# The last stage of a four-stage kernel: every engine's queue written out in the source's order, the scores one round earlier, the second layer's weights in single steps

## The chip, the cores and the metric

The kernel runs on one core of a Trainium2 chip. A core has five engines with a queue each: TensorE (PE in the profile), VectorE (DVE), ScalarE (ACT), GpSimd (POOL) and SyncE (SP), which here issues DMAs. The metric is the device time of one execution in microseconds (us). The kernel before took 1390.21 us (median of 3 runs, 1388.39 to 1392.13).

## The reference, cut to what matters

Two sequences of 1024 tokens of width 128 pass through four blocks, each added to its input after a layer norm: an attention, a mixture of experts, a second attention, and last a two-layer transformer with local attention. Only this last block is touched by the change:

```python
def _layer(x, wqkv, qs, ksc, wo, lg, lb, w1, b1, w2, b2):
    h = shift_token(x)                      # half of the features come from the token before
    q, k, v = jnp.split(h @ wqkv, 3, axis=-1)   # 8 heads of 64
    q = l2norm(q) * qs
    k = l2norm(k) * ksc
    q, k = rotary_xpos(q, k)
    o = local_attention(q, k, v)            # windows of 64, each sees itself and the one before
    x = x + o @ wo
    h = layernorm(shift_token(x)) * lg + lb
    a, g = jnp.split(h @ w1 + b1, 2, axis=-1)
    return x + (a * gelu(g)) @ w2 + b2
for l in range(2):
    x = _layer(x, ...)
```

## The kernel before

Four functions, `phase1` to `phase4`, do the four blocks. The change lies in `phase4` and in one new helper. `phase4` works on tiles of 128 tokens: 2 layers x 2 sequences x 8 tiles make 32 tiles, numbered n = 0 to 31 (`where`, L1152). A loop (L1441 to L1464) runs over rounds i; in each round a list of stages is called, each for the tile that is `late` rounds behind. One round of the list is what is called a round below.

The stages of one tile, with the lateness of each before:

- `stage_a` (0, L1159): q and k from the shifted tokens, six matmuls of 512 columns in two PSUM banks. From each bank ACT takes squares (`acc`, L1172), then DVE two products with the rotary tables (`rot` L1174 and `t` L1177).
- `stage_a1` (0, L1180): POOL adds the two products for q and for k (L1183); DVE sums the squares per head (`ss`, L1185); POOL clips them (L1186).
- `stage_a2` (1, L1189): ACT takes Ln, Exp and Square of the sums (L1193 to L1196); DVE makes the inverse norms (`rz`, `rn`, L1197 and L1198).
- `stage_b0` (2, L1201): POOL scales q and k (L1208); ACT casts k, q and a zero-padded q called Z to f16 (L1148).
- `stage_b1` (2, L1217): DVE and POOL make the f16 remainders (`q` L1222, `k` L1223); SP issues three transposing DMAs, Qz from Z, K from k, Q from q (L1229 to L1231).
- `stage_b2` (2, L1234): the values; ACT copies V (L1148), SP issues two DMAs that make a shifted copy Vs (L1245, L1247).
- `stage_c` (3, L1251): first pass of the scores, DVE takes row maxima (`mz`, L1272). ACT carries half of this tile's K into the buffer of the next tile, times a factor (L1277, called the carry below). It is absent for the last tile of a sequence.
- `stage_c2` (4): the maxima transposed into one small PSUM bank `sm`, and copied by ACT to `mT`. `stage_d` (4, L1288): the scores again, 40 small matmuls, and two Exp of ACT (`p`, L1303). `stage_e` (4, L1306): values weighted; DVE divides (L1323, L1324).
- `stage_e1` (5): the output transposed, copied by ACT (`oT`, L1333). `stage_f` (6): output projection, added by DVE to `F` (L1343).
- `stage_g` (L1345): the feed-forward part, for groups that end at the tiles in `ENDS`: seven groups of four tiles, then two of two. It is a generator: a `yield` cuts it into steps, and each `advance` runs one step of every open group. Its costly steps are the gelu (L1396, with a load of ACT's tables before and after, the latter by `exp_tables`, L68), the products (L1404), the way back (L1410 to L1417) and for the second layer a layer norm and the output.
- `stage_x` (L1074): at every fourth round the shifted, transposed tokens of four coming tiles, through the same bank `sm`: ACT and DVE take turns on it (L214, L215).

The second layer's weights and the second sequence's first layer norm are generators too (`weights` L1036, `normalize` L1028); they are put on the same list of generators as `stage_g` at rounds 12 and 4.

The order of work before: PE alone is held to the order of the source. `in_line` (L129) chains its instructions by an edge without a semaphore (`chain`, L121). ACT's table users have a chain of their own, and the carry is kept in program order. Every other instruction of DVE, ACT, POOL and SP is placed by the scheduler, which puts whatever it finds ready first.

PSUM: seven banks go round (`bank`, L1105), the eighth is `sm`.

Of the kernel before, what the change touches and what calls it, by code (L numbers as in the profile page):

```python
# [29 lines left out]
class Core:  # L30
# [98 lines left out]
    def in_line(self, f, *args):  # L129

        traced = self.nc.cur_bb.bb.instructions
        start = len(traced)
        r = f(*args)
        self.chain("line", [i for i in traced[start:] if i.engine == ENGINES[0]])
        return r
# [860 lines left out]
def phase4(k, X):  # L996
# [8 lines left out]
    with ExitStack() as es:  # L1005
# [22 lines left out]
        def normalize(b):  # L1028
            x = [X[:, NT * b + t, :] for t in range(NT)]
            mv, rstd = k.ln_stats(cp, lambda t: x[t])  # L1030
            yield
            k.ln_to(cp, [F[b][:, t, :] for t in range(NT)], lambda t: x[t], mv, rstd, scalar=b == 1)
# [3 lines left out]
        def weights(l, own, work):  # L1036

            def split(pool, name, shape, dt, src, **kw):
                w = work(shape)
                nc.sync.dma_start(w, src)  # L1040
                nc.gpsimd.tensor_scalar(w, w, WS, None, ALU.mult)
                h, lo = pool.tile(shape, dt, name=name + "h"), pool.tile(shape, dt, name=name + "l")
                nc.scalar.copy(h, w)
                nc.gpsimd.tensor_tensor(lo, w, k.f(h) if dt == F32R else h, ALU.subtract)
                return h, lo

            wq = split(own, "wq", [128, 1024], F16, A["L1_ffn_wqkv"][l][:, 0:1024])
            yield
            wv = split(own, "wv", [128, 512], F16, A["L1_ffn_wqkv"][l][:, 1024:1536])
            yield  # L1050

# [4 lines left out]
            for j in range(4):  # L1056
                nc.gpsimd.tensor_tensor(tab[:, j], tab[:, j], qs[:, j // 2, j % 2, :].unsqueeze(1).to_broadcast([128, NT, HD]), ALU.mult)
            yield
# [4 lines left out]
            w1 = split(own, "w1", [128, 6, D], F16, A["t_f1"][l])  # L1063
            col = own.tile([128, 9], F32, name="col")
            nc.sync.dma_start(col, A["t_col4"][l])
            nc.gpsimd.tensor_scalar(col[:, 0:3], col[:, 0:3], WS, None, ALU.mult)
# [26 lines left out]
        yield from weights(0, cp, work0)  # L1093
# [15 lines left out]
        class FromBank:  # L1109
            tile = staticmethod(lambda shape, dt, name: bank())  # L1110
        def from_bank(shape, dt):
            t = bank()
            if dt == F16:
                t = t.bitcast(F16)
            return t[:, :shape[1]]
        from_sm = lambda shape, dt: ps_sm.tile(shape, dt, name="sm")
        SRC = {'c2': 0, 'f': 1, 'g': 1, 'x': 0}
        src_c2 = from_bank if SRC["c2"] else from_sm
        src_f = from_bank if SRC["f"] else from_sm
        src_g = from_bank if SRC["g"] else from_sm  # L1120
        src_x = FromBank if SRC["x"] else ps_sm
# [20 lines left out]
        ENG = {'kc': 'a', 'qh': 'a', 'kh': 'a', 'z': 'a', 'oh': 'd', 'ql': 'd', 'kl': 'p', 'ul': 'd', 'gl': 'd', 'ol': 'p', 'qn': 'p', 'kn': 'p', 'uh': 'a', 'gh': 'd', 'fl': 'd', 'v': 'a', 'ra': 'p', 'rb': 'p', 'lnh': 'a', 'lno': 'd', 'mt': 'a'}  # L1142
        EDGE = {'ol': 'p', 'qh': 'a'}
        SPAN = (0, 30)
        engine = lambda n, i: ENG[n] if SPAN[0] <= i < SPAN[1] else EDGE.get(n, ENG[n])
        eng = lambda n, i=8: {"a": nc.scalar, "d": nc.vector, "p": nc.gpsimd}[engine(n, i)]
        def cpy(n, dst, src, i=8):
            (nc.scalar.copy if engine(n, i) == "a" else eng(n, i).tensor_copy)(dst, src)  # L1148

        keep = k.tc.keep_in_program_order  # L1150
# [29 lines left out]
        def stage_a1(i):  # L1180
            rot, t2, sq = S.pop(("a", i))
            for j in (1, 0):
                eng("ra" if j else "rb", i).tensor_tensor(rot[:, j], rot[:, j], t2[:, j], ALU.add)  # L1183
            ss = ep.tile([128, 2 * H], F32, name="ss")
            nc.vector.tensor_reduce(ss, sq.rearrange("p j h d -> p (j h) d"), AX.X, ALU.add)  # L1185
            nc.gpsimd.tensor_scalar(ss, ss, 1e-24 * WS**2, None, ALU.max)  # L1186
            S["a1", i] = rot, ss

        def stage_a2(i):  # L1189
            rot, ss = S.pop(("a1", i))  # L1190
            y = ep.tile([128, 2 * H], F32, name="rn")
            z = ep.tile([128, 2 * H], F32, name="rz")
            ln = nc.scalar.activation(z, ss, AF.Ln)  # L1193
            exp = nc.scalar.activation(y, z, AF.Exp, scale=-0.5)
            k.chain("tables", [ln.ins, exp.ins])
            nc.scalar.activation(z, y, AF.Square)  # L1196
            nc.vector.scalar_tensor_tensor(z, z, -0.5, ss, ALU.mult, ALU.mult)  # L1197
            nc.vector.scalar_tensor_tensor(y, z, 1.5, y, ALU.add, ALU.mult)  # L1198
            S["a2", i] = rot, y

        def stage_b0(i):  # L1201
            l, b, t = where(i)
            k0 = i % RK
            rot, rn = S.pop(("a2", i))
            rf = rot.rearrange("p j h d -> p (j h) d")
            for e, en in ((1, "kn"), (0, "qn")):
                r = slice(H * e, H * e + H)
                eng(en, i).tensor_tensor(rf[:, r, :], rf[:, r, :], rn[:, r].unsqueeze(2).to_broadcast([128, H, HD]), ALU.mult)  # L1208
# [3 lines left out]
            cpy("qh", mid(q16), pair(q), i)  # L1212
            cpy("kh", ends(k16), pair4(kk), i)
            cpy("z", ends(Z[i % 2]), pair4(q))
            S["b", i] = rot, q16, k16

        def stage_b1(i):  # L1217
            l, b, t = where(i)
# [3 lines left out]
            eng("ql", i).tensor_tensor(ends(q16), pair4(q), mid4(q16), ALU.subtract)  # L1222
            eng("kl", i).tensor_tensor(mid4(k16), pair4(kk), ends(k16), ALU.subtract)  # L1223
            if t == 0:
                nc.gpsimd.memset(K[k0][:, :, 0:64], 0.0)
            Q = sp.tile([128, H, 128], F16, name="Q", bufs=QB)
# [7 lines left out]
        def stage_b2(i):  # L1234
# [9 lines left out]
            cpy("v", V[v0][:, :, 0:HD], heads(pv), i)  # L1244
            nc.sync.dma_start(Vs[v0][64:128, :, :], V[v0][0:64, :, :])  # L1245
            if t < NT - 1:
                nc.sync.dma_start(Vs[v1][0:64, :, :], V[v0][64:128, :, :])  # L1247

        bc4 = lambda ap: ap.unsqueeze(1).to_broadcast([128, 4, 128])

        def stage_c(i):  # L1251
# [22 lines left out]
            if t < NT - 1:  # L1274
                dst = K[(i + 1) % RK][:, :, 0:64]
                if ENG["kc"] == "a":
                    keep(nc.scalar.activation(dst, K[k0][:, :, 128:192], AF.Copy, scale=fac[:, t : t + 1]))  # L1277
                else:
                    keep(nc.vector.tensor_scalar(dst, K[k0][:, :, 128:192], fac[:, t : t + 1], None, ALU.mult))

        def stage_c2(i):
            ps = src_c2([128, 128], F16)
            nc.tensor.transpose(ps, S.pop(("z", i)), k.ident16)
            mT = mTs[2] if where(i)[2] == 0 else mTs[i % 2]
            cpy("mt", mT[0:H, :], ps[0:H, :], i)
            S["m", i] = mT

        def stage_d(i):  # L1288
# [4 lines left out]
            for g in range(2):  # L1293
# [9 lines left out]
                k.chain("tables", [nc.scalar.activation(p[:, 4 * g : 4 * g + 4], st, AF.Exp).ins])  # L1303
# [32 lines left out]
        def stage_f(i):  # L1336
# [3 lines left out]
            ps = src_f([128, D], F32)  # L1340
# [4 lines left out]
        def stage_g(l, b, t0, T, last):  # L1345
# [5 lines left out]
            bank1 = bank if last else lambda: src_g([128, 512], F32)  # L1351

            def place(name, other):
                if last:
                    t = sq_place if other == "sq" else ep.tile([128, 2, H, HD], F32, name=other, bufs=3 if other == "rot" else 2)
                    return t.rearrange("p j h d -> p (j h d)")[:, :512]
                return sp.tile([128, 512], F32, name=name, bufs=1)

            tiles = lambda ap: ap[:, :n].rearrange("p (t d) -> p t d", d=D)
            hc = tiles(place("hc", "rot"))  # L1360

            ps = bank1()[:, : 64 * T].rearrange("p (t d) -> p t d", d=64)
# [11 lines left out]
            if ENG["lnh"] == "a":  # L1374
                k.ln_scalar(sp, [hc[:, t, :] for t in range(T)], mv, rstd)
            else:
                for t in range(T):
                    k.ln_apply(hc[:, t, :], hc[:, t, :], mv, rstd, t)
            yield
            yield  # L1380
            ps = bank1()
            for t in range(T):
                nc.tensor.transpose(ps[:, 128 * t : 128 * t + 128], hc[:, t, :], k.ident)
            hg = place("hc", "t2")[:, :n]
            nc.scalar.activation(hg, ps[:, :n], AF.Identity, scale=col[:, 7:8], bias=col[:, 8:9])
            gh = sp.tile([128, 512], F16, name="gh", bufs=1)[:, :n]
            gl = sp.tile([128, 512], F16, name="gl", bufs=1)[:, :n]
            nc.scalar.activation(gh, ps[:, :n], AF.Identity, scale=col[:, 7:8], bias=col[:, 8:9])
            (nc.vector if last else eng("gl")).tensor_tensor(gl, hg, gh, ALU.subtract)
            yield  # L1390
            ges = []
            for i in range(3):
# [4 lines left out]
                k.chain("tables", [gelu.ins])  # L1397
                ges.append(ge)
            k.exp_tables(gelu)
            yield  # L1400
            for i, u in enumerate(ges):
                pa = bank("g")[:, :n]
                k.mm3(pa, w1h[:, i, :], w1l[:, i, :], gh, gl)
                nc.vector.scalar_tensor_tensor(u, pa, col[:, i : i + 1], u, ALU.add, ALU.mult)  # L1404
            yield
            if not last:
                yield
            py = bank1()[:, :n]
            for i in range(3):
                nc.tensor.matmul(py, w2[:, i, :], ges[i], start=i == 0, stop=i == 2)  # L1410
            yT = place("hc", "sq")[:, :n]
            nc.scalar.activation(yT, py, AF.Identity, bias=col[:, 6:7], scale=1 / WS)
            yield
            ps = tiles(bank1())
# [230 lines left out]
```

## Time and profile before

| what | value |
|---|---|
| runs before | 1390.21 us median of 3 (1388.39 to 1392.13) |
| the profiled execution | 1389.02 us, its span 1387.2 us |
| first `rot` (L1174) of the last stage | 991.5 us |
| squares of tile 31 (L1172) start | 1309.0 us |
| Exp of tile 31 (L1303) start | 1350.5 us |
| F of tile 31 (L1343) start | 1364.9 us |
| PE, DVE, ACT, POOL busy in the whole span | 84%, 75%, 70%, 62% |

The last stage thus fills some 395 us of the span, from 991.5 us on. The time of an execution is its span and 1.8 us that lie around it. Of the views, "busy by stretches" gives each engine's busy time in a stretch of the span with the granted clock of PE, "one line" gives how often a line of the source ran, between which times and how long, and "instructions in order of time" gives start, duration, engine, line, output and input.

### The profile page before, as it was taken

The numbers are of one execution on the slowest core, as the hardware profiler recorded it, in microseconds if no ns is written. First come the engines' busy times: TensorE is split into PE (matmuls) and PEld (weight loads), VectorE is DVE, ScalarE is ACT, GpSimd is POOL, SyncE is SP. The second block draws the span as 40 slices with busy tenths as digits, with TensorE's granted clock in tenths as the row PEclk, the third lists the DMA queues.
The fourth block names the chain that finished last, engine by engine and source line by source line (L and its number), as shares of the span: only waits on it lengthen the run. The fifth ranks groups of instructions, "written<-read, shape, count | busy, mean of one in ns | idle before, by whom it ended". The sixth has DMA issues, their size and how long they took to land.

```text
span 1387.2 us, 28450 instructions
## 1 busy us (share of the span) xinstructions
PE 1159.8 (84%) x11534; PEld 729.5 (53%) x11534; DVE 1045.9 (75%) x2029; ACT 973.0 (70%) x1494; POOL 863.2 (62%) x536
## 2 busy tenths in 40 slices
PE   4789999999889687776998987689648888988986
PEld 1356666666556565544444443344325655655664
DVE  6776666876662688979978889775679887888854
ACT  2777777887667484641888876579757878887755
POOL 1666667777667363744576677576797786666611
PEclk7999999999999898987999999799959999999998
DMA  2000000010000211200000021000077755545530
GB/s 75 1 2 2 2 2 1 2 32 2 2 1 18 74 48 60 81 19 2 5 3 5 6 52 24 12 8 1 5 149 130 128 104 105 99 98 96 102 61 16
DMA packets 122530, 56.75 MB, mean 41 GB/s; under 512 B 105216, under 2 KB 114320, under 8 KB 122400
## 3 DMA queue, kind: packets, MB, share of 16 engines
q1 hardware_dynamic: 119920, 53.53, 18.3%
q8 instruction: 90, 1.47, 0.4%
q10 hardware_dynamic: 1472, 1.09, 0.3%
q0 software_dynamic: 1008, 0.33, 0.2%
q14 instruction: 40, 0.33, 0.1%
HBM read 20.99 MB, written 1.11 MB: 16 GB/s over the span
## 4 chain that ended last, share of the span: by engine, by line
PE 40%; DVE 31%; ACT 14%; POOL 6%; issue 6%; DMA 2%; SPq 0%; POOLq 0%; DVEq 0%; ACTq 0%
DVE mx L865 6%; PE big L360 5%; PE pu L49 4%; PE pu L51 3%; PE pu L50 3%; DVE nm L332 3%; ACT pt L894 2%; PE pu L916 2%; PE big L49 2%; PE big L50 2%; PE big L51 2%; DVE hl L642 1%; PE bankz L856 1%; PE bank L891 1%; DVE F L92 1%
## 5 line engine op out<-in xcount | busy, mean ns | idle before, releaser
L367 POOL TENSOR_TENSOR hl<-p,hl 128x1024 f16<-128x1024 f32 x128 | 273.9, 2143 | 139.0 <-ACT hl L366 110.9
L899 POOL TENSOR_TENSOR hl<-pt,hl 128x2048 f16<-128x2048 f32 (+1 forms) x48 | 164.7, 3435 | 102.3 <-ACT hl L898 58.9
L332 DVE TENSOR_REDUCE nm<-big 128x2 f32<-128x1024 f32 x128 | 155.1, 1219 | 31.9 <-PE big L329 31.1
L364 ACT ACTIVATE p<-big 128x1024 f32<-128x1024 f32 x128 | 130.8, 1022 | 51.9 <-PE big L360 51.1
L49 PEld LDWEIGHTS <-hl 128*128 128x128 f16 x1024 | 100.5, 98 | 73.8 <-DVE acc L392 41.2
L366 ACT CAST hl<-p 128x1024 f16<-128x1024 f32 x128 | 133.8, 1045 | 4.1
L865 DVE TENSOR_REDUCE mx<-bankz 128x1 f16<-128x512 f32 (+3 forms) x156 | 99.6, 657 | 26.3 <-PE bankz L860 19.5
L894 ACT ACTIVATE pt<-bank 128x512 f32<-128x512 f32 (+1 forms) x173 | 97.3, 601 | 26.0 <-PE bank L893 11.8
L865 DVE TENSOR_REDUCE mx<-bank 128x1 f16<-128x512 f32 (+1 forms) x148 | 94.4, 654 | 18.2 <-PE bank L860 12.5
L1208 POOL TENSOR_TENSOR rot<-rot,rn 128x512 f32<-128x512 f32 x64 | 66.9, 1066 | 61.8 <-DVE rn L1198 44.8
L49 PE MATMUL pu<-V1h,hl 128*128 128x129 f16 x512 | 92.6, 224 | 12.4 <-DVE acc L392 11.1
L50 PEld LDWEIGHTS <-hl 128*128 128x128 f16 x1024 | 101.2, 99 | 0.0
L49 PE MATMUL pu<-V0h,hl 128*128 128x129 f16 x512 | 92.8, 224 | 9.2 <-DVE acc L392 7.5
L51 PEld LDWEIGHTS <-hl 128*128 128x128 f16 x1024 | 100.3, 98 | 0.0
L894 ACT ACTIVATE pt<-bankz 128x512 f32<-128x512 f32 (+1 forms) x131 | 75.2, 597 | 35.8 <-PE bankz L893 29.4
L1183 POOL TENSOR_TENSOR rot<-rot,t 128x512 f32<-128x512 f32 x64 | 83.9, 1321 | 15.6 <-DVE t L1177 12.2
L50 PE MATMUL pu<-V0l,hl 128*128 128x129 f16 x512 | 92.1, 221 | 0.0
L51 PE MATMUL pu<-V0h,hl 128*128 128x129 f16 x512 | 92.1, 222 | 0.0
L51 PE MATMUL pu<-V1h,hl 128*128 128x129 f16 x512 | 92.0, 222 | 0.0
L50 PE MATMUL pu<-V1l,hl 128*128 128x129 f16 x512 | 92.0, 221 | 0.0
L898 ACT CAST hl<-pt 128x2048 f16<-128x2048 f32 (+1 forms) x48 | 78.4, 1634 | 10.1 <-PE pu L916 9.8
L891 PE MATMUL bank<-qst,kz 128*128 128x512 f16 (+3 forms) x222 | 66.7, 344 | 14.8 <-DVE mx L865 9.4
(418 smaller groups left out, 3797.9 us busy)
## 6 DMA issues: line engine op xcount, KB each, us to landing
sb<-sd SPq DMA_DIRECT2D x16, 512.0 KB, 4.1
Vs<-V SPq DMA_DIRECT2D x60, 130.0 KB, 2.4
work<-in_t_w SPq DMA_DIRECT2D x3, 512.0 KB, 3.6
out<-F SPq DMA_DIRECT2D x3, 256.0 KB, 2.3
X<-in_L_attn_x SPq DMA_DIRECT2D x2, 256.0 KB, 3.4
w<-in_t_wqk SPq DMA_DIRECT2D x1, 512.0 KB, 4.8
wv<-in_t_wv ACTq DMA_DIRECT2D x1, 512.0 KB, 3.7
X<-in_L_attn_x ACTq DMA_DIRECT2D x1, 512.0 KB
```

The costliest lines, as they stand in the source:

```text
L49: mm(out, lh, rh, start=start, stop=False, **kw)
L50: mm(out, lh, rl, start=False, stop=False, **kw)
L51: mm(out, ll, rh, start=False, stop=stop, **kw)
L332: S["red"] = nc.vector.tensor_reduce(S["n", u][:, i // 2, c, :], ps, AX.X, ALU.max, negate=True)
L364: S["exp"] = nc.scalar.activation(p, st, AF.Exp, scale=QSCALE**-2)
L366: nc.scalar.copy(hl[:, 0], p)
L367: S["lo"] = nc.gpsimd.tensor_tensor(hl[:, 1], p, hl[:, 0], ALU.subtract)
L865: S["max"] = nc.vector.tensor_reduce(out, ps[:, :, :n], AX.X, ALU.max, negate=True)
L891: nc.tensor.matmul(st[:, a, :w], kz[:, a0 + a, 128 * j : 128 * j + 128], q1[:, s : s + w], start=True, stop=not diag)
L894: S["exp"] = nc.scalar.activation(pt[:, a0 : a0 + m, :w], st[:, :, :w], AF.Exp)
L899: nc.gpsimd.tensor_tensor(hl[:, 1, :, :w], pt[:, :, :w], hl[:, 0, :, :w], ALU.subtract)
L1183: eng("ra" if j else "rb", i).tensor_tensor(rot[:, j], rot[:, j], t2[:, j], ALU.add)
```

## The change

A helper `in_order` takes the place of `in_line`: it chains every instruction traced by a call, on each of PE, DVE, ACT, POOL and SP, behind the one before it on the same engine. Everything that the loop calls goes through it. The loop's list is new: `stage_a2`, `stage_v` (the old `stage_b2`), `stage_c`, `stage_c2`, `stage_d`, `stage_e`, `stage_e1` and `stage_f` have other lateness or places, the casts are a stage of their own, and the carry is one (`stage_kc`). Generators get four slots per round (`gated`) for `stage_g`, two (`aside`) for the weights and the layer norm, which start at rounds 5 and 2. `stage_g` has more steps, some of them empty, and buffers of its own for every group. The scheduler's tables of engine choices (`ENG`, `SRC` and the like) go; the engines that they chose stay.

```diff
+    def in_order(self, f, *args):
+        traced = self.nc.cur_bb.bb.instructions
+        start = len(traced)
+        r = f(*args)
+        for i in traced[start:]:
+            if i.engine in ENGINES or i.engine == mybir.EngineType.SP:
+                self.chain(("order", i.engine), [i])
+        return r
...
         def normalize(b):
...
+            if b:
+                yield from k.ln_steps(cp, dst, lambda t: x[t])
+                return
...
-            def split(pool, name, shape, dt, src, **kw):
+            def split(name, shape, src):
                 w = work(shape)
                 nc.sync.dma_start(w, src)
+                yield
                 nc.gpsimd.tensor_scalar(w, w, WS, None, ALU.mult)
+                yield
...
                 nc.scalar.copy(h, w)
-                nc.gpsimd.tensor_tensor(lo, w, k.f(h) if dt == F32R else h, ALU.subtract)
+                yield
+                nc.gpsimd.tensor_tensor(lo, w, h, ALU.subtract)
+                yield
                 return h, lo
...
-                k.chain("tables", [gelu.ins])
                 ges.append(ge)
             k.exp_tables(gelu)
             yield
+            yield
+            pas = []
+            for i in range(3):
+                pas.append(bank("g")[:, :n])
+                k.mm3(pas[i], w1h[:, i, :], w1l[:, i, :], gh, gl)
+            yield
             for i, u in enumerate(ges):
-                pa = bank("g")[:, :n]
-                k.mm3(pa, w1h[:, i, :], w1l[:, i, :], gh, gl)
-                nc.vector.scalar_tensor_tensor(u, pa, col[:, i : i + 1], u, ALU.add, ALU.mult)
+                nc.vector.scalar_tensor_tensor(u, pas[i], col[:, i : i + 1], u, ALU.add, ALU.mult)
...
-        names = ("a", "a1", "a2", "b0", "b1", "b2", "c", "c2", "d", "e", "e1", "f")
-        late = (0, 0, 1, 2, 2, 2, 3, 4, 4, 4, 5, 6)
+        plan = [
+            (stage_b0, 1), (stage_v, 2), (stage_kc, 2), (stage_c2, 3), (stage_a, 0), (stage_e1, 4), (stage_d, 3),
+            (stage_a1, 0), (stage_cast, 1), (gated, 0), (stage_f, 5), (gated, 0), (stage_x, 0), (stage_c, 2),
+            (stage_b1, 1), (aside, 0), (gated, 0), (stage_a2, 0), (gated, 0), (stage_e, 3), (aside, 0),
+        ]
         i = 0
-        while i < 32 + late[-1] or gens:
-            if i == 4:
-                gens.append(normalize(1))
+        while i < 32 + 5 or gated:
             if i == 2:
+                aside.append(normalize(1))
                 own = es.enter_context(k.pool("p4v", 1, "right"))
-            if i == 12:
-                gens.append(weights(1, own, lambda shape: ep.tile(shape, F32, name="t2")))
-            for step in ("b0", "a2", "b2", "c2", "a", "e1", "d", "a1", "gated", "f", "x", "c", "gated", "e", "b1"):
...
+            if i == 5:
+                aside.append(weights(1, own, lambda shape: own.tile(shape, F32, name=f"w{shape[1]}")))
+            for f, late in plan:
+                n = i - late
...
```

With the new list each queue's order within round i is: PE: v(i-2), c2(i-3), a(i), e1(i-4), d(i-3), f(i-5), x, c(i-2), e(i-3). ACT: copy of V(i-2), the carry of tile i-2, `mT` of i-3, two squares of i, `oT` of i-4, two Exp of i-3, the casts k, q, Z of i-1, then x, then Ln, Exp, Square of i. DVE: `rot`, `t` twice and `ss` of i, F of i-5, x, `mz` of i-2, remainder of q of i-1, `rz`, `rn` of i, `ri`, `u` of i-3. POOL: scaling of i-1, two adds and the clip of i, remainder of k of i-1. SP: Vs of i-2, then Qz, K, Q of i-1. The first `gated` slot lies behind the casts, the second behind f, the third behind the remainders, the fourth behind `rz` and `rn`. A group that ends at tile n begins at round n+5 in the third slot with its shifted input; statistics are in the fourth; in round n+6 its layer norm, its transposes and the f16 split of its input; in round n+7 the gelu in the first slot, the other products' matmuls in the third and the products in the fourth; in round n+8 the way back, with the second layer's layer norm and output reaching into round n+9. `stage_x` falls in round n+8 of a group of four.

## The prediction

> **What bounds the kernel now.** I first read busy by stretches, cut at the starts of `ss` (L1185), of which each round has one: rounds 4 to 9, which hold no feed-forward work, rounds 14 to 18, a full cycle of four with one group in it, and the drain from round 31 on.
>
> ```profile
> 1037.65:1079.95 42.30, 35.96 (x557) 25.89 (x556) 38.08 (x78) 32.34 (x77) 33.28 (x34) 0.96 0.69 123
> 1133.14:1176.27 43.13, 36.50 (x476) 23.57 (x476) 35.61 (x81) 34.37 (x74) 29.02 (x31) 1.00 0.56 107
> 1312.44:1387.20 74.76, 55.80 (x610) 39.19 (x608) 41.04 (x132) 42.59 (x74) 14.95 (x20) 0.92 0.20 41
> ```
>
> The columns are the stretch, its length, then busy us of PE, PE's weight loads, DVE, ACT and POOL, the granted clock, the DMAs' share and GB/s. In the cycle PE, DVE and ACT are each busy for 34 to 37 of 43 us: no one engine bounds it, and the idle sixth is what a better order could win. Next, one line, L1185, in two windows: 5 bare rounds in 42.3 us, 8.46 us each, and 22 rounds in 232.5 us, 10.57 us each.
>
> ```profile
> L1185 DVE TENSOR_REDUCE ss<-acc x6: 1200/1208/1211, 1037.6 to 1079.9; 128x16 f32<-128x1024 f32 x6
> L1185 DVE TENSOR_REDUCE ss<-acc x23: 1200/1207/1211, 1079.9 to 1312.4; 128x16 f32<-128x1024 f32 x23
> ```
>
> PE's order is already the source's, so the gain must come from the other four queues. The change issues the same instructions and DMAs as before, in another order; nothing but waits can change, and the question is how long a round becomes when each queue waits in order. The group's own buffers and the empty steps I cost at nothing: no wait on such a buffer is among the 60 longest of the stage.
>
> **The wait that the change adds.** The carry (L1277) moves from behind `stage_c`, lateness 3, to near the head of ACT's round at lateness 2. It needs K of tile i-2, which SP issued in the round before. Behind the waiting carry stand, on ACT, `mT`, both squares, `oT`, both Exp and three casts; the scores of PE, `rot` and `t` of DVE, POOL's adds and SP's next Qz and K wait for these. Before, the carry hardly ever waited (3.1 us on K's DMA from 1040 to 1330 us, by the groups of lines) since the scheduler put it where it was ready. So a loop closes from one carry to the next, and the instructions in order of time price it. On ACT (start, duration):
>
> ```profile
> 1185.01 0.61 ACT L1148 CAST k<-rot 128x512 f16<-128x512 f32 x1
> 1185.52 0.59 ACT L1303 ACTIVATE p<-b 128x512 f32<-128x512 f32 x1
> 1186.01 0.61 ACT L1148 CAST q<-rot 128x512 f16<-128x512 f32 x1
> 1186.52 0.62 ACT L1148 CAST Z<-rot 128x512 f16<-128x512 f32 x1
> ```
>
> 512 columns follow each other every 0.5 us. Carry 0.65, `mT` 0.15, squares 1.0, `oT` 0.5, Exp 1.0, casts k and q 1.0, Z 0.6: Z ends 4.9 us after the carry starts. SP's rows, and from the view of tile K the time from issue to landing:
>
> ```profile
> 1187.16 1.23 SPq L1229 DMA_TRANSPOSE Qz<-Z  x1
> 1188.49 1.29 SPq L1230 DMA_TRANSPOSE K<-k  x1
> DMA to landing us min/median/max: 3.0/3.2/4.4
> ```
>
> Qz goes first and holds SP 1.33 us, then K lands 3.2 us after its issue: 4.9 + 1.33 + 3.2 = **9.4 us per round**. The same loop through DVE and POOL:
>
> ```profile
> 1224.50 0.69 DVE L1174 TENSOR_TENSOR rot<-b,tab 128x512 f32<-128x512 f32 x1 [0.30 <-ACT acc L1172]
> 1225.11 0.68 DVE L1177 TENSOR_TENSOR t<-b,tab 128x512 f32<-128x512 f32 x1
> 1225.87 0.68 DVE L1174 TENSOR_TENSOR rot<-b,tab 128x512 f32<-128x512 f32 x1
> 1226.47 0.67 DVE L1177 TENSOR_TENSOR t<-b,tab 128x512 f32<-128x512 f32 x1
> ```
>
> `rot` starts only when ACT's square of the same bank has ended (the releaser in brackets). Carry and `mT` 0.8, first square 0.6, four products 2.6, the second add 1.28 (L1183's median), clip 0.25, remainder of k 1.16 (L1223's), landing 3.2: 9.9 us. POOL's adds come before its remainder of k in the new list, so this path counts. I take **9.9 us for a bare round**, bounds 9.4 and 10.2 (with L1183 at its longest, 1.73). That is 1.4 more than the 8.46 of before. A tile that ends a sequence has no carry; the next rounds, 9, 17 and 25, then go on at ACT's and DVE's own pace, 0.9 us sooner each by my count.
>
> **What a group of four adds.** Nothing, if all of it lies in ACT's 5 us between Z and the next carry. Three things do not fit.
>
> Round n+7, the gelu in order on ACT behind the casts, ahead of Ln of the new tile:
>
> ```profile
> 1239.28 1.28 ACT L1396 ACT_TABLE_LOAD   x1
> 1240.58 1.84 ACT L1396 ACTIVATE ge<-b,col 128x512 f32<-128x512 f32 x3
> 1242.44 1.28 ACT L73 ACT_TABLE_LOAD   x1
> ```
>
> 4.9 + 4.4 + 0.75 (Ln, Exp, Square, 0.25 each) + 0.5 (V) = 10.6 before the next carry can start: 0.7 over 9.9. And DVE's `rn` waits for that Square at 10.1; behind it are 0.45 for `rz` and `rn`, 2.1 for three products (L1404, 0.7 each), 1.1 for `ri` and `u`: `u` ends at 13.7, 3.1 into the next round. There `oT` waits for it: 0.6 for the transposes, 1.5 for the scores, 0.65 for Exp, 1.6 for casts, 1.33 and 3.2 for Qz and K make a round of 12.0, 2.1 over.
>
> Round n+8, `stage_x`: ACT and DVE take turns on `sm`, and DVE's maxima, remainder, `rn`, F and `u` stand behind these turns. I count `u` ending 3.4 us into the following round, which by the same sum makes that one 12.2 long, and 0.5 to 0.7 on rounds n+6 and n+8 themselves. All together 0.7 + 2.1 + 2.3 + 1.2, and 0.7 for PE's early matmul of the way back, are 7.0 us per four rounds at worst; 0.7 at best, if DVE's lateness is taken up each time. Between these ends I take **4**, since the 2.8 of the gelu come from rows without slack and the rest rests on my order of small pieces. PE's stall at `sm` of before (about 3 us in a cycle) is gone by the new order of c2 and x, but PE has room in these rounds and gives nothing of it back.
>
> The table loads were weighed against the Trainium skill. The page ScalarE: Activation LUTs, section What ACT_TABLE_LOAD costs, puts a drain of about 1380 ns behind each load of 1283 ns. The rows above show the load at 1.28 us and the next instruction 0.02 us behind it. With the page's drain the gelu round would be 2.8 us longer, some 16 us in six rounds; the rows decide.
>
> **Start, weights, drain.** ACT's order now puts the cast of Z of tile 0 and the copy of V ahead of the squares of tiles 2 and on. These tiles' buffers come free late:
>
> ```profile
> 1022.90 1.07 ACT L1148 COPY V<-b 128x512 f32<-128x512 f32 x2 [1.32 <-DVE X L210]
> 1024.62 1.00 POOL L1137 MEMSET Z<- 128x1024 f16 x1
> ```
>
> The pools in front of them don't change, so I keep these times: Z is cast at 1025.7 to 1026.3, Qz issued till 1027.6, K lands at 1030.8, first carry at 1031, squares of tile 2 at 1031.8 (before at 1005.5; tile 4 followed at 1034.6). That costs about two rounds of head start, of which one comes back as the scores are a round earlier. The second layer's weights have 17 steps in rounds 5 to 13, with 17 us of POOL work that fits its free 3 to 4 us per round; ACT's three casts wait for POOL and may hold a carry: +2 us, bounds 0 and 6, in place of a like cost at rounds 12 and 13 (13.0 and 12.6 us apart).
>
> The sum: first carry 1031; rounds 2 to 7, 6 x 9.9 = 59.4; rounds 8 to 30, 23 x (9.9 + 4/4) = 250.7; minus 3 x 0.9; plus 2: carry of round 31 at 1340.4, squares of tile 31 at 1341.2 against 1309.0, **+32**. The drain has a round less: from these squares to the last Exp 41.5 us before; after, I count 36 (no new tiles, but the lateness of DVE goes along), so -6, bounds 0 and -16. From the last Exp to the end, 36.7 us before, the same chain of three last groups runs. 1387.2 + 32 - 6 = 1413 in the span, 1415 with the 1.8 around it, and the runs' median lies 1.2 above the profiled execution: **1416 us**.
>
> Bounds of this case: with 0.7 per group instead of 4, -19, and 1397; with 7.0, +17, and 1433; bare rounds at 10.2 add a little more, weights and drain +-6. So 1395 to 1438.
>
> **Rivals.** (1) *The round is as long as its loop and no longer*, faster. If the loop is 9.4 to 9.5 us (POOL's path hidden), groups add nearly nothing and the drain gives its full 16: 1031.8 + 29 x 9.5 - 2.7 = 1304.6, -4, -16: about 1370, from 1362 to 1386. For it: three engines have a sixth of their time free, and 10.57 us per round with groups is above the loop. Against it: bare rounds ran at 8.46 and can only lose, and the gelu rows. It decides below 9.65 us per round on average; a chance of 0.27. (2) *Gains and losses cancel* at about 10.0 us per round with half the drain's gain: 1390, 0.05. (3) *The edges bind little*, as the scheduler had chosen nearly this order: 1389. Against it: SP issued Qz before K at 1187 and after it at 1196, and POOL ran a table of the second layer at 1017. 0.03. (4) *My forecast*, slower by the carry's wait on K: 0.65.
>
> The range of 8 in 10 takes the forecast's own 1395 to 1438 and reaches down to 1370. Faster by over 0.3% (4 us, about what a measurement of this kernel can tell from no change) has 0.27, the same 0.08, slower 0.65.
>
> **What the profile after would show.** Right: ACT's carry idle before it on K's DMA in most rounds, by 1 to 5 us; `ss` 9.9 us apart in bare rounds; rounds n+8 and n+9 of a group of four near 12; `u` of a gelu round behind `rn`, and `rn` behind the second table load; squares of tile 2 not before 1030. Wrong: `ss` under 9.4 apart on average, the carry not waiting, or Z's memory free long before 1022, which would bring the whole stage forward by up to 20 us.

## The result, and the profile after

The changed kernel takes **1456.61 us** (median of 4 runs, 1451.5 to 1457.59) against 1391.17 us for the kernel before (4 runs, 1388.39 to 1392.2): ratio 1.0466, 95% interval 1.0437 to 1.0496. The forecast was 1416 us, with 1438 as the upper end. It had the direction, and 40 us too little. The profiled execution took 1457.59 us, its span 1455.8.

Busy by stretches, after: the bare rounds (squares of tile 2 to those of tile 6), a cycle of four rounds with one group, and the drain. Columns as in the prediction.

```profile
1019.39:1061.31 41.92, 27.18 (x341) 16.35 (x335) 32.50 (x73) 25.35 (x62) 23.55 (x23) 0.84 0.53 103
1248.87:1294.88 46.01, 39.09 (x491) 25.17 (x490) 34.78 (x80) 35.15 (x74) 25.65 (x26) 1.00 0.47 93
1379.78:1455.80 76.02, 53.17 (x536) 37.67 (x534) 39.48 (x125) 36.77 (x67) 15.47 (x21) 0.89 0.19 41
```

The cycle is 2.9 us longer than the 43.13 of before with the same work in it: DVE and ACT are busy for 35 us in both. The four bare rounds take 10.5 us each, of which PE is busy for 6.8. One line, `ss` (now L1180), after, in the bare rounds and from there to the end of the tiles:

```profile
L1180 DVE TENSOR_REDUCE ss<-acc x5: 1201/1207/1208, 1022.4 to 1064.3; 128x16 f32<-128x1024 f32 x5
L1180 DVE TENSOR_REDUCE ss<-acc x26: 1205/1206/1208, 1064.3 to 1384.2; 128x16 f32<-128x1024 f32 x26
```

Before, 22 rounds took 232.5 us, 10.57 each; now 25 rounds, from tile 6 to tile 31, take 319.9 us, 12.8 each (the same 25 took 260.3 us before). They are not alike: 8 of them, from tile 6 to tile 14, take 117.7 us. In that stretch the second layer's weights are loaded, and POOL in order of time shows four instructions with long idle times before them (in brackets, with what ended them):

```profile
1064.65 2.77 POOL L1056 TENSOR_SCALAR w<-w 128x1024 f32<-128x1024 f32 x1 [7.37 <-DMA w<-in_L_ffn_wqkv]
1093.05 1.50 POOL L1056 TENSOR_SCALAR w<-w 128x512 f32<-128x512 f32 x1 [9.46 <-DMA w<-in_L_ffn_wqkv]
1123.64 1.26 POOL L1080 TENSOR_TENSOR tab<-tab,qs 128x512 f32<-128x512 f32 x1 [11.94 <-DMA tab<-in_c_rope]
1153.92 2.13 POOL L1056 TENSOR_SCALAR w<-w 128x768 f32<-128x768 f32 x1 [9.72 <-DMA w<-in_t_f]
```

POOL stood 38.5 us in all at these four, with the scaling and the adds of the next tile behind. SP in order of time shows why: the load of the first of these weights stands behind all three transposes of its round, and only half a round ahead of the multiply.

```profile
1057.31 1.23 SPq L1230 DMA_TRANSPOSE K<-k  x1
1058.63 1.29 SPq L1231 DMA_TRANSPOSE Q<-q  x1
1059.97 0.57 SPq L1054 DMA_DIRECT2D w<-in_L_ffn_wqkv  x1
```

Issued at 1059.97, used at 1064.65. The start of the stage went the other way, with ACT in order of time:

```profile
1012.55 0.62 ACT L1213 CAST Z<-rot 128x512 f16<-128x512 f32 x1 [0.81 <-POOL Z L1142]
...
1018.77 0.72 ACT L1254 ACTIVATE K<-K,fac 128x512 f16<-128x512 f16 x1 [4.51 <-DMA K<-k]
1019.39 1.07 ACT L1168 ACTIVATE acc<-b 128x512 f32<-128x512 f32 x2
```

Z is cast 13 us sooner than forecast, and the carry then stands 4.51 us for K's DMA. From 1030 to 1400 us 13 of 25 carries (now L1254) waited for K, 23.1 us in all, where it had been 3.1 us before (1040 to 1330 us). From 1175 us on it was five of 17, 8.2 us in all.

### The profile page after: what moved, and what is told of

The parts are those of the page before. It is cut to its first block, busy times and chain, and to the rows that moved or that the text cites. A ratio compares the mean times of both kernels' runs of the same rounds, so it can differ in the third digit from the quotient of the medians.

```text
span 1455.8 us, 28372 instructions
## 1 busy us (share of the span) xinstructions
PE 1182.0 (81%) x11534; PEld 737.0 (51%) x11534; DVE 1054.4 (72%) x2029; ACT 976.1 (67%) x1494; POOL 857.2 (59%) x536
## 5 line engine op out<-in xcount | busy, mean ns | idle before, releaser
L875 DVE TENSOR_REDUCE mx<-bankz 128x1 f16<-128x512 f32 (+3 forms) x156 | 99.3, 657 | 26.3 <-PE bankz L870 19.5
L1203 POOL TENSOR_TENSOR rot<-rot,rn 128x512 f32<-128x512 f32 x64 | 67.1, 1069 | 66.5 <-DVE rn L1195 61.3
L49 PE MATMUL pu<-V1h,hl 128*128 128x129 f16 x512 | 92.6, 224 | 12.4 <-DVE acc L402 11.7
L88 POOL TENSOR_TENSOR ln_rstd<-ln_rs,nhalf 128x4 f32<-128x4 f32 (+2 forms) x30 | 35.5, 1185 | 91.6 <-DVE ln_rs L84 50.2
```

What stands on the lines that cost most here:

```text
L49: mm(out, lh, rh, start=start, stop=False, **kw)
L875: S["max"] = nc.vector.tensor_reduce(out, ps[:, :, :n], AX.X, ALU.max, negate=True)
L1203: nc.gpsimd.tensor_tensor(rf[:, r, :], rf[:, r, :], rn[:, r].unsqueeze(2).to_broadcast([128, H, HD]), ALU.mult)
```

## The experiments

Each `us` of the first sixteen is one execution beside one of the kernel before on the same chip (1395.4 for the first four, 1388.9 for the next four, 1386.1 and 1390.6 for the last two fours); six executions of one kernel lay between 1392.7 and 1399.5, so a few us of a single one say nothing, and "less before", the difference to the kernel before on the same chip, is the safer column. Starts of `ss` cut each run into stretches: the start of tile 6, tiles 6 to 14, tiles 14 to 31, and from there to the end of the span (the drain).

| run | us | less before | tile 6 at | 6 to 14 | 14 to 31 | drain |
|---|---|---|---|---|---|---|
| before | 1389.0 | | 1052 | 81.0 | 179.3 | 74.8 |
| after | 1457.6 | +65 (medians) | 1064 | 117.7 | 202.2 | 71.6 |
| e1 | 1443.7 | +48.2 | 1066 | 102.0 | 201.5 | 72.7 |
| e2 | 1471.2 | +75.8 | 1055 | 114.8 | 215.0 | 84.9 |
| e3 | 1394.6 | -0.8 | 1071 | 82.0 | 178.4 | 61.3 |
| e4 | 1512.9 | +117.5 | 1076 | 123.9 | 224.3 | 87.1 |
| e5 | 1434.6 | +45.6 | 1066 | 92.7 | 201.7 | 72.9 |
| e6 | 1427.5 | +38.6 | 1054 | 86.6 | 201.1 | 83.5 |
| e7 | 1425.2 | +36.3 | 1054 | 88.4 | 201.0 | 79.7 |
| e8 | 1436.7 | +47.8 | 1062 | 110.7 | 201.2 | 60.9 |
| e9 | 1422.6 | +36.5 | 1069 | 92.1 | 198.4 | 60.9 |
| e10 | 1409.9 | +23.8 | 1055 | 85.3 | 198.2 | 69.8 |
| e11 | 1419.3 | +33.2 | 1051 | 86.6 | 205.2 | 74.6 |
| e12 | 1425.8 | +39.7 | 1065 | 93.2 | 201.3 | 64.4 |
| e13 | 1416.8 | +26.3 | 1072 | 86.5 | 195.9 | 61.1 |
| e14 | 1411.2 | +20.6 | 1059 | 102.9 | 185.9 | 61.7 |
| e15 | 1406.0 | +15.4 | 1066 | 80.9 | 190.0 | 67.7 |
| e16 | 1397.4 | +6.9 | 1072 | 82.8 | 183.3 | 57.7 |

**e1: the weights' loads all at once**, in round 5, first used two rounds later; nothing else moved.

```diff
+            if l:
+                early["wq"] = load([128, 1024], A["L1_ffn_wqkv"][l][:, 0:1024])
+                early["wv"] = load([128, 512], A["L1_ffn_wqkv"][l][:, 1024:1536])
+                early["w1"] = load([128, 6, D], A["t_f1"][l])
+                rest()
+                for _ in range(4):
+                    yield
```

> The changed kernel, but the loads of the second layer's weights are all issued in round 5, two rounds ahead of the first use, instead of half a round ahead. Theory A (POOL, now in order, stands at the head of its queue until each load lands: 7.4 + 9.5 + 11.9 + 9.7 = 38 us of idle time in the profile after, most of which the whole stage waits out): 25 to 35 us less than the changed kernel's 1457, so 1422 to 1432. Rival B (the weights' own work on POOL and ACT stretches these rounds, not the wait): 1450 or more.

A miss of both ranges: it gave back 13 us (17 by the differences to before). POOL no longer waits for a weight, but SP now stands for 6.85 us on one issue, with Qz and K of the next tile behind it (SP in order of time, e1):

```profile
1064.36 6.85 SPq L1086 DMA_DIRECT2D wo<-in_L_ffn_wo  x1
...
1073.55 1.32 SPq L1250 DMA_TRANSPOSE Qz<-Z  x1
```

**e2: the scores one round later**, as before the change, so that the carry follows K by a round more.

```diff
-            (stage_b0, 1), (stage_v, 2), (stage_kc, 2), (stage_c2, 3), (stage_a, 0), (stage_e1, 4), (stage_d, 3),
+            (stage_b0, 1), (stage_v, 2), (stage_kc, 3), (stage_c2, 4), (stage_a, 0), (stage_e1, 5), (stage_d, 4),
...
-            (stage_a1, 0), (stage_cast, 1), (gated, 0), (stage_f, 5), (gated, 0), (stage_x, 0), (stage_c, 2),
+            (stage_a1, 0), (stage_cast, 1), (gated, 0), (stage_f, 6), (gated, 0), (stage_x, 0), (stage_c, 3),
...
-            (stage_b1, 1), (aside, 0), (gated, 0), (stage_a2, 0), (gated, 0), (stage_e, 3), (aside, 0),
+            (stage_b1, 1), (aside, 0), (gated, 0), (stage_a2, 0), (gated, 0), (stage_e, 4), (aside, 0),
```

> The changed kernel, but the carry, both passes of the scores, the values, the output projection and what follows them come one round later in the list, as before. Theory A (the carry waits for K's transfer that was issued half a round before, and with it ACT): bare rounds fall from 9.9 us to 8.3 to 8.8, ACT's carry no longer waits for the transfer, and the time falls by 5 to 15 us net of one more round in the drain: 1442 to 1452. Rival C (DVE's and ACT's order alone sets the round, the carry waits in their shadow): bare rounds stay at 9.9 us, and the extra round costs 8: 1465.

A miss, slower than the change by 15 us (10 by the differences). The carry waits for no DMA any more, tile 6 comes 10 us sooner, and the four rounds from tile 2 to tile 6 take 34.7 us instead of 41.9. But all groups start a round later too, so that `stage_x` falls in the gelu's round, which grows to 17.0 us. The carry's wait is thus a price in bare rounds; what it costs in the others e2 can't tell.

**e3: the new list with PE alone in order**, ACT's table users in a chain of their own and the carry in program order, as before the change.

```diff
-            if i.engine in ENGINES or i.engine == mybir.EngineType.SP:
+            if i.engine == ENGINES[0]:
```

> The changed kernel with its new list and steps, but only PE's instructions are chained in the source's order, with the old chain for the users of ACT's tables and the carry in program order; DVE, ACT, POOL and SP are placed by the scheduler. Theory A (the order of the four queues costs the time): 1385 to 1405. Rival D (the new list, its lateness or the new buffers cost it whatever the order): 1435 or more.

As fast as before (one execution of each, -0.8 us). The list and the lateness cost nothing in sum: the 65 us lie in the order of the four other queues. Its stretches differ from those of before all the same: tile 6 comes 19 us later and the drain is 13.5 us shorter. In e3 the second layer's weights are loaded from 1013 us on and most of POOL's work on them lies between 1018 and 1046 us, ahead of tile 6.

**e4: the list of before with five queues in order**, with double buffers for `hc`, `gh` and `gl` and own ones for all groups.

```diff
-        self.chain("line", [i for i in traced[start:] if i.engine == ENGINES[0]])
+        for i in traced[start:]:
+            if i.engine in ENGINES or i.engine == mybir.EngineType.SP:
+                self.chain(("order", i.engine), [i])
```

> The kernel before with its old list, but all five queues chained in the source's order, and every group of the feed-forward part with two sets of buffers of its own. Theory A (an order by source needs steps that are cut where they wait, so the old list does worse than the new one): 1470 to 1550. Rival D (the new list is what costs): 1400 to 1430.

Slower still: the change's list is the better of the two for queues in order.

**e5: the loads spread**, one or two at a time over rounds 3 to 6, used after all are issued.

```diff
+                early["wq"] = load([128, 1024], A["L1_ffn_wqkv"][l][:, 0:1024])
+                yield
+                early["wv"] = load([128, 512], A["L1_ffn_wqkv"][l][:, 1024:1536])
+                yield
...
-            if i == 5:
+            if i == 3:
                 aside.append(weights(
```

> As the run with early weights, but the loads go out one or two at a time from round 3 to round 6, not eight in a row. In that run SP stood 6.9 us on the issue of one load with many short pieces behind a megabyte of others, and Qz and K behind it, and round 6 to 7 stayed 16.7 us long. Theory A: that round falls to about 12 and the time to 1433 to 1438. Rival: the round is long for another reason, 1443.

As expected. POOL waits for no weight, the stretch from tile 6 to 14 falls from 117.7 to 92.7, and the others stay within 1.4 us. **The late loads of the weights cost the change 25 us of this stretch**, 23 us of the span (20 by the differences to before). The load of `wo` holds SP for 0.58 us here.

**e6: e5, scores one round later, and `stage_x` in the round in which a group begins**, apart from the gelu (the diff shows this last edit). **e7: the gelu behind Ln, Exp and Square** besides, by three more `yield` before it, and `stage_x` one round before the one of the change.

```diff
-                    if i % 4 == 3 and i + 1 < 32:
-                        l, b, t = where(i + 1)
+                    if i in {1: 4, 7: 8, 9: 12, 13: 16, 17: 20, 21: 24, 25: 28}:
+                        l, b, t = where({1: 4, 7: 8, 9: 12, 13: 16, 17: 20, 21: 24, 25: 28}[i])
```

> Scores, values and what follows one round later (as in the second run), the weights' loads spread, and the shifted tokens of the coming tiles made in the round in which a group begins, not in that of its gelu. Theory A (the second run lost by that collision, 17 us in one round of four, not by the lateness; the carry's wait on the transfer is a true cost): four rounds fall from 48 to 49.5 us to 43 to 44, bare rounds stay at 7.4 to 9.4, 1405 to 1420. Rival C (the lateness itself brings nothing, the four rounds take 46 as in the changed kernel): 1435 or more.

> As the run before, with the gelu and its two table loads put behind Ln, Exp and Square of the same round on ACT instead of ahead of them, and the rest of the group one round later; the shifted tokens one round later too. Theory A (DVE's inverse norms, the products and the values' division stand behind the second table load): another 2 to 3 us per four rounds, 1390 to 1408. Rival E (ACT has no room wherever the gelu stands): as the run before.

Both missed; e7 came out as its rival had it. The four bare rounds take 32 us (33 in e7) instead of 44, with no wait of the carry, but tiles 14 to 31 take 201 us as in e5. In rounds with a group these moves gave nothing; each run moved more than one thing, so a gain and a loss may hide each other.

**e8: ACT and DVE free**, PE, POOL and SP in order.

```diff
-            if i.engine in ENGINES or i.engine == mybir.EngineType.SP:
+            if i.engine in (ENGINES[0], ENGINES[3], mybir.EngineType.SP):
```

> The changed kernel with PE, POOL and SP in the source's order, and ACT and DVE placed by the scheduler (ACT's table users chained, the carry in program order). Splits the 60 us by queue. If ACT's and DVE's order costs what the rounds with a group lose (about 1 us a round) and POOL's and SP's what the weights lose: 1415 to 1430. Rival F (POOL's order is all of it, through the scaling that waits for the inverse norms): 1445 or more.

Between its two ranges. Of the span 20.8 us come back: 10.7 in the drain, 7.0 at the weights, 2 before tile 6, and 1 in tiles 14 to 31.

**e9 to e12: the output's transposes (`stage_e1`) behind the projection**, on e5, e6 and e7, and on e5 with the late gelu (the diff is e9's).

```diff
-            (stage_b0, 1), (stage_v, 2), (stage_kc, 2), (stage_c2, 3), (stage_a, 0), (stage_e1, 4), (stage_d, 3),
-            (stage_a1, 0), (stage_cast, 1), (gated, 0), (stage_f, 5), (gated, 0), (stage_x, 0), (stage_c, 2),
+            (stage_b0, 1), (stage_v, 2), (stage_kc, 2), (stage_c2, 3), (stage_a, 0), (stage_d, 3),
+            (stage_a1, 0), (stage_cast, 1), (gated, 0), (stage_f, 5), (stage_e1, 4), (gated, 0), (stage_x, 0), (stage_c, 2),
```

> The run with spread weights, with the transpose of the attention's output (and ACT's copy of it, oT) moved from ahead of the second pass of the scores to behind the output projection. New theory G, from the chain of the profile after: in rounds with a group one chain runs through three engines, u at the end of DVE's round, transpose and scores on PE, oT, Exp, casts, the group's work and the norm's Ln, Exp, Square on ACT, then rz, rn, the group's work and u on DVE again; in it ACT's and DVE's work for the group add up one after the other. Moving the transpose takes u out of it: four rounds fall from 46 us to 42 to 43, the time by 15 to 22 us, 1412 to 1420. Rival H (DVE's own load sets these rounds): 1430 or more.

> The same move in the list that is one round later with the shifted tokens apart, where the carry waits for no transfer. Theory G: four rounds fall from 47.4 us to 41 to 43, bare rounds stay at 7.4 to 8.3, 1395 to 1408. Rival H: 1420 or more.

> The same move in the list with the gelu behind the norm. Theory G: with u no longer in the chain, the norm ahead of the gelu takes the second link, from the table loads to the products, out too: 1385 to 1400, the first list in order near the kernel before. Rival H: 1418 or more.

> The changed kernel's lateness, spread weights, the gelu behind the norm and the output's transpose behind the projection. Theory G with the carry's loop of 9.4 to 9.9 us left as the only one: 32 rounds near 9.9 to 10.3, 1395 to 1410. Rival H: 1425 or more.

Two near misses (e9, e10) and two misses (e11, e12), which came out where rival H had put them. The gain of e9 and e10 (12 and 18 us of the span) came, but in the wrong place for its reason: the chain from `u` through `oT` and the scores should have shortened the rounds with a group, and 12 to 14 us of it lie in the drain, only 3 in tiles 14 to 31. e10 is the best of the kernels with five queues in order, 24 us slower than before.

**e13 and e14: PE and POOL in order, PE and SP in order**, to split what e8 left.

> The new list with PE and POOL in the source's order; DVE, ACT and SP left to the scheduler. With PE alone it took 1394.6 us, with PE, POOL and SP 1436.7. Theory J (the two queues cost it together: POOL stands at a weight that SP issues late, so SP's freedom to issue the loads early takes most of it away): 1397 to 1412, and POOL waits for the weights' DMAs by under 10 us in all. Theory P (POOL's order by itself: POOL stands at the reciprocal roots of the group's layer norm and at the scaling of the next tile, with the next work behind it, whoever issues the loads): 1418 to 1437.

> The new list with PE and SP in the source's order; DVE, ACT and POOL free. Theory J: 1397 to 1412, since POOL takes other work while a load is on its way. Theory P: SP's order costs next to nothing, 1392 to 1402. Rival S (SP's order costs most of the 42 us, since Qz, K, Q and the loads wait for each other in its queue): 1420 to 1437.

Neither theory holds as it was put: over e3, POOL's order costs 27.1 us by itself, SP's 21.5, and both together (e8) 48.6, each from one execution. By stretches of the span (from its start to the `ss` of tile 14, and on from there), over e3:

| run | to tile 14 | 14 to 26 | 26 to 30 | 30 to the end | sum |
|---|---|---|---|---|---|
| e13 (POOL) | +5.0 | +5.3 | +13.3 | -1.3 | +22.2 |
| e14 (SP) | +8.8 | +2.9 | +4.9 | +0.1 | +16.6 |
| e8 (both) | +19.8 | +13.9 | +8.7 | -0.2 | +42.2 |
| after (all) | +28.9 | +11.2 | +10.4 | +12.4 | +63.0 |

Tiles 6 to 14 alone take 102.9 us in e14 against 82.0 in e3, but tile 6 comes 12.1 us sooner, since e3 has its work on the weights ahead of it. With that work in the stretch and SP free (e13) it takes 86.5. POOL is free in e14 and waits for the loads only 7.7 us (POOL's waits, 1058 to 1162 us); the loads stand as late in SP's queue as in the change.

```profile
POOL w L1056 <- DMA w<-in_L_ffn_wqkv: 7.7, 2, 5.2
```

What POOL's order costs from tile 26 to 30 can be seen in its waits (total, times, longest), from 1160 to 1350 us in e3, then in e13, and from 1175 to 1390 us after the change:

```profile
POOL rot L1204 <- DVE rn L1196: 38.1, 17, 3.7
POOL rot L1182 <- DVE t L1173: 24.1, 10, 5.0
POOL ln_rstd L88 <- DVE ln_rs L84: 4.8, 3, 3.4
```

```profile
POOL rot L1204 <- DVE rn L1196: 42.0, 12, 5.9
POOL ln_rstd L88 <- DVE ln_rs L84: 24.2, 5, 9.6
POOL rot L1182 <- DVE t L1173: 12.9, 8, 5.8
```

```profile
POOL ln_rstd L88 <- DVE ri L1324: 19.9, 5, 8.4
```

The group's layer norm takes one power of four numbers in each row on POOL (`ln_rstd`). In order, POOL stands at it with the scaling of the next tile behind it; free, it takes other work until the sums are there. From tile 14 to 26 these waits are 2 to 3 us, one in four rounds. The long ones, 6.8 and 9.6 us in e13, 8.4 and 4.8 us after the change, lie between tile 26 and 30, the only rounds up to tile 30 with two such powers.

**e15 and e16: the lists of e10 and e9 with PE alone in order.**

> Only PE in order, on the list of the experiment with scores one round later, weights' loads spread, the shifted input in the round in which a group begins and the output's transposes behind the projection (1409.9 us with five queues in order). If five orders cost there what they cost on the list of the change (62 us), 1348. If the list's own repairs removed most of what the orders cost, so that the orders cost 10 to 25 there: 1385 to 1400. I expect 1380 to 1395, at or a little under the kernel before.

> Only PE in order, on the list with the loads spread and the output's transposes behind the projection, at the lateness of the change (1422.6 us with five queues in order). If the scores one round later matter only to a queue that waits in order: as with all moves, within 5 us of it. If PE's order itself profits from the later scores: 5 to 15 us above it. I expect 1383 to 1395.

Both missed, e16 by 2 us. The four orders cost 30 us on e9's list and 8 on e10's, but e10's list is itself 16 us worse than the change's under a free order.

**e17 and e18: order at the start only.** Rounds 0 to 2, or 0 and 1, with five queues in order and nothing of later rounds ahead of them; then as e3.

```diff
-            if i.engine == ENGINES[0]:
+            if i.engine == ENGINES[0] or self.round <= 2:
...
+            elif ("order", i.engine) in self.last:
...
+                self.tc.add_manual_dep(i, self.last["order", i.engine].name, dep, reason="chain")
```

> All five queues in order in rounds 0 to 2 only, and nothing of a later round may go ahead of them; from round 3 on PE alone is in order, as in the run that took 1394.6 us. With five queues in order the first carry came at 1018.8 us and the squares of tile 3 some 8 us sooner than with PE alone, since no work of the last stage goes ahead of the end of the stage before it on POOL and DVE. If that head start is kept: 1394.6 - 8, 1380 to 1388, under the kernel before. Rival (the head start is given back, since a freer order meets the same waits a little later): 1391 to 1398.

> The same with rounds 0 and 1 in order only. If the head start comes from what is kept out of the end of the stage before it, round 2 need not be in order: within 3 us of the other run, 1380 to 1388. If tile 2's own place in the order matters: 1388 to 1396.

Neither came under the kernel before: e17 came out as its rival had it, e18 0.4 us above its second range. They took 1396.11 and 1396.43 us against 1388.55, ratios 1.0053 (1.0035 to 1.007) and 1.0058 (1.0044 to 1.0072). In e17 tile 3 came 6 us sooner than in e3, and tile 6 was 6 us later again: PE stood 14.0 us at the scores for a K (the waits of PE, 1040 to 1085 us, e17).

```profile
PE b L1275 <- DMA K<-k: 14.0, 1, 14.0
```

No kernel tried beats the one before.

## Why the prediction was wrong

Its own sum beside the profile after, by starts of the squares:

| stretch | forecast | measured | difference |
|---|---|---|---|
| to tile 2 | 1031.8 | 1019.4 | -12.4 |
| tiles 2 to 6 (4 x 9.9) | 39.6 | 41.9 | +2.3 |
| tiles 6 to 14 (8 x 9.9, 6 x 1 for groups, -0.9, +2) | 86.3 | 117.7 | +31.4 |
| tiles 14 to 31 (17 x 10.9, -1.8) | 183.5 | 200.8 | +17.3 |
| drain (78.2 - 6) | 72.2 | 76.0 | +3.8 |
| sum | 1413.4 | 1455.8 | +42.4 |

**The step that failed: "17 us of POOL work that fits its free 3 to 4 us per round", weights +2, bounds 0 and 6.** It priced a queue in order by the engine's busy time and put the wait of the instruction at its head at nothing. Four steps of POOL follow the issue of their load by 4.0 to 7.7 us, on a queue of SP that issues its transposes first, and POOL stood 38.5 us. e5 issues the loads earlier, which takes this wait away, and gives back 25 of the 31.4 us. How the loss splits between POOL's order and SP's is not settled: with POOL free, SP's order by itself (e14) still loses time at the weights. None of my bounds held this, and it decides by itself that the range was missed: without the 25, about 1432, and e5 took 1434.6.

**A group of four, "I take 4" between 0.7 and 7.0, was mis-sized.** A cycle measured 46.0 us against my 43.6: 10.1, 10.1, 12.8 and 13.0 by `ss`, which is 6.4 over four rounds of 9.9, near my worst bound. From tile 14 to 26 the rounds took 137.7 us by `ss` against my 129.0. The four from tile 26 to 30 took 51.8 against 43.6, and there I had priced no more than anywhere, though a second `ln_rstd` falls in them. The chain of after has the gelu's round as I had put it, only longer:

```profile
1274.42 0.52 ACT Z L1213
1274.96 1.28 ACT L1386
1276.25 1.84 ACT ge L1386 x3
1278.11 1.28 ACT L73
1279.41 0.22 ACT rz L1191
...
1280.43 0.17 DVE rn L1195
1280.61 1.98 DVE ge L1397 x3
...
1283.25 0.44 DVE u L1325
1283.73 0.44 PE b L1332 x2
```

From the carry (1269.14) to the next is 11.7 us (I had 10.6), to the end of `u` 14.5 (13.7). It reads like the cause, and I took it for it in e7 and e9 to e12. e8 says otherwise: with ACT and DVE free this chain is not bound to its order, and tiles 14 to 31 take 201.2 us still. Of the 23.8 us that this stretch lost over e3, e13 has 17.5 with POOL's order, for which I had counted nothing in a group, but 13.3 of them from tile 26 to 30. From tile 14 to 26 POOL's and SP's orders cost 5.3 and 2.9 us alone and 13.9 together. Not settled: ACT and DVE in order with POOL and SP free was not run, so this chain may be a second bound of nearly equal length behind POOL's; and POOL's `ln_rstd` was not moved by itself.

**The carry was right in size and wrong in reach.** "9.9 us for a bare round" measured 10.5 on average (9.8, 12.2, 10.0 and 9.9 by `ss`), and e6 without that wait 8.0; but bare rounds are six of thirty. In the rounds with groups the carry seldom waited, and e6, where it never does, is no faster there than e5 (201.1 and 201.7 us). The prediction let it set every round.

**The start, "the pools in front of them don't change, so I keep these times", failed** to the good side by 12 us. The pools don't, but their last users do: with POOL and DVE in order less work of the last stage goes ahead of the tail of the stage before it, whose last reciprocal root ran at 1008.84 us instead of 1017.33 in e3. I had named this as what would prove me wrong. e17 and e18 show that the gain is not kept under a free order. Without this error in its favour the forecast would have lain 53 us too low, not 40. The 1005.5 us that the prediction gives for the squares of tile 2 before are those of tile 3 (tile 2's start at 999.9); its sum doesn't use them.

**The drain**, -6 with bounds 0 and -16, measured -2.2. Freeing ACT and DVE (e8) makes it 11 us shorter, and moving the output's transposes with all queues in order (e9 against e5) 12 us. In the direction, and in the table loads at 1.28 us with nothing behind them, the prediction held.

Of the rivals, the faster one fell at its own condition: rounds ran at 12.8 us, not under 9.65. "The edges bind little" fell with e3.

## What to carry to other kernels

Price a queue in order by who stands at its head and for how long, one queue at a time, and the queues with spare busy time above all: POOL at 59% and SP cost 49 of these 65 us. Put a load well ahead of its use (two rounds and more in e1 and e5; half a round cost 25 us here), and not behind the transfers that the next round waits for. And free one engine's order at a time before repairing a list: that told in four runs (e3, e8, e13, e14) what six repairs of the list had not.

## What the runs showed of the hardware

The issue of one DMA does not have one price. The load of the second layer's `wo` held SP for 0.57 us before the change (at 1010.22 us), 3.91 us after it, behind the loads of `qs` and the tables, 6.85 us in e1, behind five other loads, and 0.58 us in e5, where the loads are spread. What makes it so was not measured by itself.

PE's granted clock was lower where PE stood more: 0.96 in the bare rounds of before with PE busy for 35.96 of 42.30 us, and 0.84 after with 27.18 of 41.92; back to 1.00 in a cycle with 39.09 of 46.01. The busy share alone does not give it: it is 0.85 in the first and in the last of these. Whether the lower clock costs time there, where PE waits, no run tells apart.

The Trainium skill, ScalarE: Activation LUTs, What ACT_TABLE_LOAD costs, adds some 1380 ns of drain to a load of 1283 ns for every switch of tables. The trace does not show it: after the change, too, the load starts 0.02 us behind the cast ahead of it, takes 1.28 us, and the gelu starts 1.29 us after its load does.
